# fc2, w1 and w2 of a two-layer image network with seven block products instead of eight (Strassen's method), on one core

## The chip, the cores, the metric

One core of a Trainium2 chip; the program runs on it alone. The metric is the time of one execution on the device, in microseconds (us), of fp32 work throughout. Each run is compared with the kernel before as it ran in the same rounds; from one set of rounds to another that kernel's median lay between 3582.13 and 3584.61 us. The granted clock is the share of full speed that the profile shows for TensorE's clock. A ratio is the mean time of one kernel's fast runs over that of the other's of the same rounds, so it is not quite the ratio of the medians that are quoted.

## What is computed

Eight images of 384 channels and 32x32 pixels pass through two layers: an attention block with a two-matrix MLP, then a ConvNeXt block (7x7 depthwise convolution, layernorm, w1, Gelu, global response normalization GRN, w2). Cut to what matters:

```python
h   = gelu(einsum('bnc,oc->bno', layernorm(x1), w_fc1) + b_fc1)     # 384 -> 1536
x2  = x1 + einsum('bnh,oh->bno', h, w_fc2) + b_fc2                  # fc2: 1536 -> 384
y   = depthwise_7x7(x2);  y = layernorm(y over channels)
y   = gelu(einsum('bhwc,cd->bhwd', y, w1) + b1)                     # w1: 384 -> 1536
gx  = sqrt(sum(y**2 over pixels));  nx = gx / (mean(gx) + eps)
y   = gamma * (y * nx) + beta + y                                   # GRN
out = x2 + einsum('bhwd,dc->bhwc', y, w2) + b2                      # w2: 1536 -> 384
```

## The kernel before

Activations lie with channels on the 128 partitions and 1024 pixels (two halves of 512) along them. A product is one matmul of a 128x128 weight tile with 128x512. Products are written to PSUM tiles of one or two banks; in this program each bank of a tile takes one 128x512 result. fc2, w1 and w2 have 72 such products per image each. A small scheduler (`Flow`) interleaves the instruction streams while the program is written: `flow.pe(us)` tells it how long TensorE will be busy, and side chains (`yield us`) put their next instructions behind so much TensorE work. Every engine then runs its instructions in the order in which they were written; semaphores are set by the framework from what each instruction reads and writes. The stages run in this order for image b: query/key, attention, fc1, fc2 of image b; w1 of image b-1; values of b+1; w2 of b-1. VectorE does the convolution beside all of it.

```python
ps_s = tile_pool("ps_s", bufs=2, PSUM)     # tiles of two banks
ps_o = tile_pool("ps_o", bufs=4, PSUM)     # tiles of one bank
...
def linear(lhsT, rhs, nk, name, done=None):
    ps = ps_s.tile([P, N], F32, tag="s", name=name)          # both halves, two banks
    for k in range(nk):
        for h in range(2):
            nc.tensor.matmul(out=ps[:, half(h)], lhsT=lhsT(k), rhs=rhs(k)[:, half(h)], start=(k == 0), stop=(k == nk - 1))
        flow.pe(2 * U)
    return ps
...
# fc2
for ct in range(CT):
    ps = linear(lambda k: weights.at(wb, k)[:, ct * P : (ct + 1) * P], lambda k: hid[:, k, :], HT, ...)
    nc.vector.scalar_tensor_tensor(xt[:, ct, :], ps, col("bfc2", ct), xt[:, ct, :], ALU.add, ALU.add)
...
# w1
for m in range(HT):
    ps = linear(lambda k: w[:, k, :], lambda k: acc[:, k, :], CT, f"h_{b}_{m}")
    nc.scalar.activation(y[:, m, :], ps, AF.Gelu, bias=b1[:, m : m + 1])
    nc.scalar.activation(ps, y[:, m, :], AF.Square, accum_out=gx[:, m : m + 1])
...
# GRN: the scale goes into w2's rows
nc.scalar.activation(gx, gx, AF.Sqrt)
yield 3.5
nc.tensor.matmul(out=ps[:, :HT], lhsT=ones, rhs=gx, start=True, stop=True)      # gxsum
```

## Time and profile before

| | before |
|---|---|
| median of the runs beside the changed kernel | 3584.61 us (3578.94 to 3587.52, 4 runs) |
| TensorE busy, profiled run | 3498.2 of 3582.0 us, mean granted clock 0.991 |
| one inner image, query/key to query/key | 435.9 us |
| fc2, w1, values, w2 of it | 67.8, 62.7, 16.0, 61.8 us |

The stages are read from the timeline of TensorE: from the first product of one stage to the first of the next. fc2 is longer than w2 because the small column sums of the layernorms stand in it (six or seven of 0.86 us).

### The profile page before, as it was taken

What the parts mean: (1) busy time and instruction counts of PE and PEld (TensorE: products, weight loads), DVE (VectorE), ACT (ScalarE), POOL (GpSimd) and SP (SyncE); (2) the same over time, 40 slices, a digit from 0 to 9 for tenths busy, and PEclk for the clock granted to TensorE, in tenths of its full rate; (3) what the DMA queues carried; (4) which work ended last, traced back from release to release, by engine and by line L of the source; (5) the groups of instructions that cost most, each with busy time, mean ns of one, the idle gap of its engine ahead of it and who ended that gap; (6) DMA issues with size and microseconds to landing.
All of it is one profiled execution on the core that took longest, in us unless ns stands there. A gap on an engine that the chain in (4) does not pass through costs nothing.

```text
span 3582.0 us, 35524 instructions
## 1 busy us (share of the span) xinstructions
PE 3498.2 (98%) x14358; PEld 1475.7 (41%) x14358; DVE 1908.0 (53%) x2151; ACT 1242.5 (35%) x1501; POOL 452.6 (13%) x280
## 2 busy tenths in 40 slices
PE   8999999999999999999999999999999999999978
PEld 3344334443344433444334443444434444344433
DVE  2113795376821768128671376613775247839931
ACT  3541543405424054240542415423153322532130
POOL 1001022100211002200121001120011200224000
PEclk9999999999999999999999999999999999999989
DMA  3012001220012200122002220021201212022110
GB/s 112 13 30 88 17 16 44 84 62 22 16 44 91 61 20 12 50 88 59 19 16 62 72 65 13 24 77 50 65 13 33 89 40 54 16 62 83 53 42 30
DMA packets 93036, 170.56 MB, mean 48 GB/s; under 512 B 29376, under 2 KB 29504, under 8 KB 92736
## 3 DMA queue, kind: packets, MB, share of 16 engines
q1 hardware_dynamic: 92288, 165.73, 16.0%
q8 instruction: 115, 1.88, 0.2%
q10 hardware_dynamic: 576, 2.48, 0.2%
q14 instruction: 57, 0.47, 0.0%
HBM read 133.03 MB, written 25.43 MB: 44 GB/s over the span
## 4 chain that ended last, share of the span: by engine, by line
PE 90%; DVE 7%; POOL 1%; ACT 1%; DMA 0%; issue 0%; SPq 0%; DVEq 0%; POOLq 0%
PE fc L267 13%; PE o L461 12%; PE o L252 12%; PE h L252 12%; PE fc L252 12%; PE s L441 12%; PE qk L252 7%; DVE wqkv L621 5%; PE v L370 4%; PE proj L384 3%; PE ln_var L305 1%; PE ln_sum L290 1%; POOL ln_a L287 1%; DVE acc L621 1%; ACT L274 0%
## 5 line engine op out<-in xcount | busy, mean ns | idle before, releaser
L621 DVE SCALAR_TENSOR_TENSOR acc<-pad,vec,acc 128x1024 f32<-128x1024 f32 x1008 | 1277.1, 1333 | 0.0
L450 ACT ACTIVATE p<-s 128x1024 f32<-128x1024 f32 x512 | 522.6, 1023 | 399.7 <-PE s L441 399.6
L441 PE MATMUL s<-qk 48*64 48x512 f32 x4096 | 537.9, 594 | 12.2 <-ACT p L450 10.7
L461 PE MATMUL o<-p,v 64*64 64x512 f32 x4096 | 533.5, 592 | 0.0
L252 PE MATMUL o<-y,w 128*128 128x512 f32 x1152 | 501.4, 597 | 3.8 <-issue 3.8
L267 PE MATMUL fc<-xn,fc 128*128 128x512 f32 x1152 | 500.6, 593 | 0.0
L252 PE MATMUL fc<-hid,fc 128*128 128x512 f32 x1008 | 441.2, 592 | 0.0
L252 PE MATMUL h<-acc,w 128*128 128x512 f32 x1008 | 437.2, 593 | 0.0
L428 POOL TENSOR_TENSOR attn<-attn,r 128x512 f32<-128x512 f32 x48 | 95.8, 1995 | 1931.5 <-DMA r<-back 1667.2
L252 PEld LDWEIGHTS o<-y,w 128*128 128x128 f32 x1152 | 220.8, 192 | 280.7 <-issue 274.1
L267 PEld LDWEIGHTS fc<-xn,fc 128*128 128x128 f32 x1152 | 218.2, 190 | 278.2 <-issue 273.2
L252 PEld LDWEIGHTS fc<-hid,fc 128*128 128x128 f32 x1008 | 191.5, 190 | 241.1 <-issue 241.1
L252 PEld LDWEIGHTS h<-acc,w 128*128 128x128 f32 x1008 | 190.7, 190 | 235.8 <-issue 235.8
L441 PEld LDWEIGHTS s<-qk 48*64 48x64 f32 x4096 | 153.0, 133 | 308.3 <-issue 273.2
L461 PEld LDWEIGHTS o<-p,v 64*64 64x64 f32 x4096 | 157.1, 133 | 287.8 <-issue 283.5
L546 ACT ACTIVATE hid<-fc,bfc_f 128x512 f32<-128x512 f32 x192 | 131.8, 686 | 372.4 <-PE fc L267 372.3
L354 ACT ACTIVATE qk<-qk,bqk 128x1024 f32<-128x1024 f32 x48 | 53.5, 1114 | 570.9 <-PE qk L252 570.9
L252 PE MATMUL qk<-xn,wqkv 128*128 128x512 f32 x576 | 248.6, 592 | 0.0
L647 ACT ACTIVATE y<-h,b_f 128x1024 f32<-128x1024 f32 x96 | 106.9, 1113 | 290.6 <-PE h L252 257.0
L402 DVE TENSOR_TENSOR attn<-o,attn 128x512 f32<-128x512 f32 x64 | 44.1, 688 | 295.8 <-ACT attn L400 295.8
L621 DVE SCALAR_TENSOR_TENSOR wqkv<-pad,vec,wqkv 128x416 f32<-128x416 f32 (+1 forms) x288 | 191.5, 740 | 0.0
L252 PEld LDWEIGHTS qk<-xn,wqkv 128*128 128x128 f32 x576 | 109.4, 190 | 137.1 <-issue 136.6
(129 smaller groups left out, 1974.9 us busy)
## 6 DMA issues: line engine op xcount, KB each, us to landing
fc<-in_wfc SPq DMA_DIRECT2D x108, 384.0 KB
w<-in_w SPq DMA_DIRECT2D x96, 384.0 KB
xn<-in_x SPq DMA_DIRECT2D x16, 768.0 KB
x<-in_x SPq DMA_DIRECT2D x16, 768.0 KB
kept<-x SPq DMA_DIRECT2D x8, 1536.0 KB
res<-kept SPq DMA_DIRECT2D x48, 256.0 KB
out_y<-res SPq DMA_DIRECT2D x48, 256.0 KB
r<-back SPq DMA_DIRECT2D x96, 96.0 KB
```

Of the source, the lines that this page charges most:

```text
L252: nc.tensor.matmul(out=ps[:, half(h)], lhsT=lhsT(k), rhs=rhs(k)[:, half(h)], start=(k == 0), stop=(k == nk - 1),)
L267: nc.tensor.matmul(out=ps, lhsT=lhsT(k), rhs=rhs(k)[:, half(h)], start=(k == 0), stop=(k == nk - 1))
L354: nc.scalar.activation(parts[:, i, m, :], ps, AF.Identity, bias=bqk[:, at : at + 1], scale=1.0 if i else SCALE)
L370: nc.tensor.matmul(out=ps[:, :C], lhsT=xn[:, k, t * P : (t + 1) * P], rhs=wv_sb[:, k, :], start=(k == 0), stop=(k == CT - 1),)
L384: nc.tensor.matmul(out=ps, lhsT=wproj_sb[:, m, ct * P : (ct + 1) * P], rhs=attn[:, m, :], start=(m == 0), stop=(m == CT - 1),)
L428: nc.gpsimd.tensor_tensor(attn[:, m, :], attn[:, m, :], r, ALU.mult)
L441: nc.tensor.matmul(out=s[64 * i : 64 * i + 64, j, :], lhsT=kT[64 * j : 64 * j + HD, m, k0 : k0 + 64], rhs=qT[64 * j : 64 * j + HD, m, half ...
L450: nc.scalar.activation(p, s, AF.Exp)
L461: nc.tensor.matmul(out=outs[i][64 * j : 64 * j + 64, :], lhsT=v[keys, t, at : at + 64], rhs=p[keys, j, :], start=(t == 0), stop=(t == KT - 1),
L546: nc.scalar.activation(hid[:, m, half(h)], ps, AF.Gelu, bias=bias[:, m : m + 1])
L621: nc.vector.scalar_tensor_tensor(dst, window, tap, dst, ALU.mult, ALU.add)
L647: nc.scalar.activation(y[:, m, :], ps, AF.Gelu, bias=b1[:, m : m + 1])
```

## The change

Two by two blocks are multiplied with seven products in place of eight (Winograd's form): sums of weight blocks S1 to S4 and of activation blocks T1 to T4 are made first, the products are added up after. The third row tile of fc2 and w2 and the third input tile of w1 stay straight. Weight sums of fc2 and w1 are made once in image 0 and kept in DRAM; those of w2 are made for each image, as GRN scales the weights. Done for seven of eight images. T1, T3, T4 are made on GpSimd (for w1 on VectorE), T2 and all sums out of PSUM on VectorE. The core of the diff (exact path, weight order, preparation and pacing cut):

```diff
+    def down(hid, t1, weights, wname, first, add, done, name):          # fc2 and w2
+        def banks(i):
+            ps = ps_s.tile([P, 2, NH], F32, tag="s", name=f"{name}_{i}")
+            return ps[:, 0, :], ps[:, 1, :]
+        straight = banks(0)                                             # A31, A32: 24 products
+        ...
+        making_t3 = flow.spawn(differences(t3, b22, b12), paced=True)   # GpSimd
+        p1, p2 = banks(1)
+        product(p1, "A11", b11)
+        nc.scalar.copy(u2, p1)
+        for k in range(h):
+            nc.vector.tensor_tensor(t2[k], b22[k], t1[k], ALU.subtract)
+        product(p2, "A12", b21)
+        first(0, 0, p2); add(0, 0, u2); done(0, 0)
+        making_t4 = flow.spawn(after(making_t3, differences(t4, b21, t2)), paced=True)
+        p5, p6 = banks(2)
+        product(p5, "S1", t1)
+        first(1, 1, p5); first(0, 1, p5)
+        product(p6, "S2", t2)
+        nc.vector.tensor_tensor(u2, p6, u2, ALU.add)
+        p3, p7 = banks(3)
+        product(p3, "S4", b22)
+        add(0, 1, p3); add(0, 1, u2); done(0, 1)
+        product(p7, "S3", t3)
+        ...
     def grn_up(b, acc, weights, tag, fold):                              # w1, pair (i, j = i + 6)
-            ps = linear(lambda k: w[:, k, :], lambda k: acc[:, k, :], CT, f"h_{b}_{m}")
-            nc.scalar.activation(y[:, m, :], ps, AF.Gelu, bias=b1[:, m : m + 1])
-            nc.scalar.activation(ps, y[:, m, :], AF.Square, accum_out=gx[:, m : m + 1])
+            if fold:
+                fold_b1(i, (a11, a12, a13)); fold_b1(j, (a21, a22, a23))
+            p12 = ps_s.tile([P, 2, NH], F32, tag="s", name=f"h_{b}_{i}")
+            accumulate(p12[:, 0, :], [(a11, b11)])
+            nc.scalar.copy(c21, p12[:, 0, :])
+            accumulate(p12[:, 1, :], [(a13, b31), (a12, b21)])
+            plus(c11, p12[:, 1, :], c21)
+            p5 = product((s1, t1))
+            plus(c21, product((s2, t2)), c21)
+            plus(c12, p5, c21)
+            plus(c12, product((s4, b22), (a13, b32)), c12)
+            finish(i)                                                    # Gelu on ScalarE
+            plus(c21, product((s3, t3)), c21)
+            plus(c22, p5, c21)
+            plus(c21, product((a23, b31), (a22, t4)), c21)
+            plus(c22, product((a23, b32)), c22)
+            finish(j)
+            first_difference(y1, y, i)                                   # T1 of w2, GpSimd
+            for m in (i, j):
+                nc.scalar.activation(squares, y[:, m, :], AF.Square, accum_out=gx[:, m : m + 1])   # squares: p12
-                start_conv(b, 1.55 if b == B - 2 else 1.8)
+                start_conv(b, 1.5 if b == B - 2 else 1.75, 10)
-                    after(state["norm3"], both(xn, xn, eps0, "g1", f"ln1_{b + 1}", True), 0 if b else 6)
+                    after(state["norm3"], both(xn, xn, eps0, "g1", f"ln1_{b + 1}", True, adder=nc.vector), 0 if b else 6)
```

## The prediction

> **What bounds the kernel now.** I read the page first, then the chain of waits, then groups, then the chain in order of time over one inner image. The span and busy lines:
>
> ```profile
> span 3582.0 us, 35524 instructions
> PE 3498.2 (98%) x14358; PEld 1475.7 (41%) x14358; DVE 1908.0 (53%) x2151; ACT 1242.5 (35%) x1501; POOL 452.6 (13%) x280
> PE 90%; DVE 7%; POOL 1%; ACT 1%; DMA 0%; issue 0%; SPq 0%; DVEq 0%; POOLq 0%
> ```
>
> TensorE is busy 98% and holds 90% of the chain that ended last: time is TensorE time. The only long stretch of the chain on VectorE lies near the end (about 3217 to 3441 us, the last image's convolution), which the change leaves as it is. The chain in order of time shows one inner image nearly seamless:
>
> ```profile
> 1107.63 53.22 PE h L252 x124
> 1160.84 3.87 PE v L370 x12
> 1164.71 0.04 issue
> 1164.75 0.39 PE gxsum L662 x2
> 1165.14 11.71 PE v L370 x36
> 1176.86 61.80 PE o L252 x144
> 1238.65 30.91 PE qk L252 x72
> ```
>
> x144 in 61.80 us: one record is 0.429 us, and an fp32 product of 128x128 by 128x512 leaves two records, so it costs **0.858 us**. The image lasts 435.9 us (first query/key product to the next, 802.79 to 1238.65); some 500 such products are 429 us, so only about 7 us are not products. A saved product is worth its whole 0.858 us, as long as nothing new makes TensorE wait; there is hardly any old wait behind which a new one could hide.
>
> [...] The first two lines are VectorE's timeline without and with a GpSimd sum beside it, the third is that sum:
>
> ```profile
> 513.11 2.47 DVE L621 SCALAR_TENSOR_TENSOR acc<-pad,vec,acc 128x1024 f32<-128x1024 f32 x2
> 529.04 3.48 DVE L621 SCALAR_TENSOR_TENSOR acc<-pad,vec,acc 128x1024 f32<-128x1024 f32 x2
> 529.21 2.24 POOL L286 TENSOR_TENSOR ln_a<-x 128x512 f32<-128x512 f32 x1 [4.62 <-DVE x L392]
> ```
>
> Two taps took 2.47 us alone and 3.48 us with it: each GpSimd sum takes 1.0 us from VectorE, and takes itself 2.2 us instead of the 1.3 us of the quiet rows. [...]
>
> ```profile
> L402 DVE TENSOR_TENSOR attn<-o,attn 128x512 f32<-128x512 f32 x64 | 44.1, 688 | 295.8 <-ACT attn L400 295.8
> L286 DVE TENSOR_TENSOR ln_t<-xn 128x512 f32<-128x512 f32 x1 | 0.7, 691 | 12.0 <-DMA xn<-in_x 12.0
> L647 ACT ACTIVATE y<-h,b_f 128x1024 f32<-128x1024 f32 x96 | 106.9, 1113 | 290.6 <-PE h L252 257.0 <-DVE b_f L641 33.5
> L648 ACT ACTIVATE h<-y 128x1024 f32<-128x1024 f32 x96 | 98.6, 1027 | 3.1
> L274 ACT ACT_TABLE_LOAD x47 | 60.3, 1283 | 3.1 <-issue 2.3
> L428 POOL TENSOR_TENSOR attn<-attn,r 128x512 f32<-128x512 f32 x48 | 95.8, 1995 | 1931.5 <-DMA r<-back 1667.2
> L621 DVE SCALAR_TENSOR_TENSOR acc<-pad,vec,acc 128x1024 f32<-128x1024 f32 x1008 | 1277.1, 1333 | 0.0
> ```
>
> In a row I take 0.64 us per sum (three similar ones from L294 stand in 1.87 us). [...] here a load is 1.28 us (L274).
>
> **The change, part by part.**
>
> *Removed.* fc2 goes from 72 products to 66 per image (row tile 2 straight 24, seven block products of 6), w2 likewise, w1 from 72 to 66 (11 instead of 12 for each pair of row tiles, six pairs). Each is done for seven of eight images: fc2 for images 0 to 6, w1 and w2 for 0 to 5 and 7. 3 x 7 x 6 = 126 products x 0.858 = **108 us**, the most there is to win (3.0%).
>
> *w1, VectorE and ScalarE beside it.* A pair now takes 11 x 0.858 = 9.44 us of TensorE. It brings eight VectorE sums out of PSUM (8 x 0.64 = 5.1 us), one ScalarE copy (0.58), two Gelu (1.11 each) and two squares (1.03 + 0.19). By order on each engine they form a loop: copy 0.58, eight sums 5.1, second Gelu 1.11, two squares 2.44, then the next pair's copy: 9.3 us with four handovers of 0.05 us, against 9.44. So TensorE still just leads, with about 0.3 us to spare: of the four banks, the sixth product takes the one that the sum of S2T2 frees about 6.6 us into the pair, and TensorE wants it at 6.87. Four banks are not simply taken in turn (in the attention, two are held while the projection takes three), so p5, held long, need not block. But what norm1 puts into the loop shows: two VectorE sums (1.4 us) and Ln, Exp and two table loads (3.9 us) in the first pair, part of it in idle time. I count 1.5 us for each of six images: **9 us**.
>
> *Wait at the GRN sum.* TensorE issues the gxsum product 3.87 us after w1's last product (lines above). Today ScalarE is just ready: Gelu 1.1, square 1.2, table 1.28, root 0.21 = 3.8. Afterwards: last sum 0.7, Gelu 1.1, two squares 2.4, table 1.28, root 0.21 and handovers = 6.2. New wait 2.4 us x 7 = **17 us**.
>
> *Folding b1, once.* In the first w1 stage each pair now starts with two column sums whose operands VectorE makes (three operations, 1.0 us) after the former pair's last sum: 0.75 + 1.0 + 0.2 + 0.2 + 0.16 + 1.0 + 0.2 = 3.5 us of standing for each of six pairs, 21 us. Folding costs today 9 us (87.6 us from w1's start to w2's in the first image against 78.7 in the next). Net **12 us**. The new preparation of sums in image 0 lies beside an attention with VectorE nearly idle; I allow **3 us**.
>
> *fc2.* GpSimd gets 12 differences (T3, T4), some 1.3 to 2 us each, among norm3's sums; VectorE the six of T2 and 13 sums out of PSUM. The block products wait for nothing: T2 has five microseconds of A12 and five of S1 before it is read, T3 25, T4 30. What can wait is the small layernorm product between them, placed 3 us after its GpSimd sums were issued: the second half's sum of squares falls among T3. I count 2 us for six images: **12 us**.
>
> *w2.* VectorE has per stage of 56.6 us: taps at a pace of 2.28 us (25 x 1.21 = 30 us), seven scalings and sums of 128x768 (0.9 each, 6.3), T2 4.1, thirteen sums 8.7, and 13 us lost to GpSimd: 62 us. It ends some 6 us behind. The banks of S3T3 are what the next stage's first product needs, with 5.1 us between: about 1.2 us x 6 = **7 us**.
>
> *Weights.* 33 loads instead of 24 per image; the page shows DMA engines at 1 to 3 tenths, and w1's tenth chunk is asked for 28 us before its use. Nothing. *Clock:* waits of 1 to 4 us are too short to show here; the granted clock was 0.991.
>
> Sum: 108 - 9 - 17 - 12 - 3 - 12 - 7 = 48 us; 3587 - 48 = **about 3540 us**, 1.3% faster.
>
> **Rivals.** (a) *The loop becomes w1's bound.* If a sum takes its whole 0.69 us and a handover 0.1, the loop is 9.9 us instead of 9.44: another 3 us per stage, and each intrusion counts fully, some 4 us; over seven stages 40 us more. For: the spare time is 0.3 us. Against: neighbours in the trace overlap. It would give 3575 to 3585, no gain. (b) *All is hidden.* The pacing (slow taps at first, norm1's sums moved to VectorE) looks measured; if fc2 and w2 run without a wait and w1 loses only the gxsum wait and the fold, 108 - 29 = 79 us: 3508. For: T2, T3, T4 have slack, and the taps can catch up under the query/key products. Against: two of the terms follow from order alone. (c) [...] With 20 more GpSimd sums under a running convolution, taps end late and norm3 starts late, so fc2 waits: 5 to 10 us an image, 3580 to 3610. Against: 147 taps at a pace of 1.75 us and the slow start make 273 us, and from w1's end to fc2 there are some 293 us of products.
>
> **Range and chances.** The terms I hold firm are 108 saved, 17 and 12 lost. The others (31 us) may vanish or double; (a) adds 40. So 3498 to 3595 for 8 in 10. Below 3515 (2%) needs nearly all of the soft terms to vanish: 0.25. Slower by 2% (3659) would take more than all that is saved plus 72 us: 0.03. Within 2%: 0.72.
>
> **What would show it.** Products on TensorE: 126 fewer, 252 records. w1's stage near 59 to 60 us against 62 (without the layernorm product), its mean idle time released by VectorE; gxsum waits for ScalarE's root by 2.4 us an image; in the first w1 stage, the column sums wait for VectorE, some 20 us in all; w2 57 us with VectorE full and a short wait at the first query/key product. I am wrong if w1 takes over 63 us (rival a), if fc2 waits long for GpSimd or for the end of the convolution (c), or if gxsum and fold waits aren't there.

## The result, and the profile after

The changed kernel takes **3878.89 us** (3875.0 to 3878.92, 4 runs); ratio to the kernel before 1.082, 95% interval 1.0802 to 1.0839. It is 8% slower where I had forecast 1% faster. The page of the changed kernel, busy line and chain by engine:

```profile
span 3877.0 us, 36414 instructions
PE 3534.3 (91%) x14106; PEld 1463.2 (38%) x14106; DVE 2492.5 (64%) x2769; ACT 1262.9 (33%) x1551; POOL 872.5 (23%) x504
PE 75%; DVE 16%; ACT 5%; issue 1%; POOL 1%; DMA 1%; SPq 0%; DVEq 0%; POOLq 0%; ACTq 0%
```

The products are gone as counted: 14358 - 14106 = 252 records. But TensorE is busy for 36 us **longer**, and idle (span less busy) for 343 us instead of 84: 259 + 36 = 295 us. With 108 us of products gone, 36 us longer means that the products that are left take 144 us more than before. VectorE and ScalarE have come onto the chain. What TensorE waited for, longest first in total (the wait, us in total, times, the longest):

```profile
PE h L316 <- ACT y L810: 134.6, 42, 6.1
...
PE o L316 <- DVE res L921: 32.0, 7, 9.9
PE fc L316 <- DVE x L690: 28.9, 7, 4.8
PE b L222 <- DVE w_lnb L218: 24.3, 12, 5.5
PE gxsum L874 <- ACT gx L871: 20.7, 8, 5.7
```

The first line was in no rival of mine. 42 is once for each of the six pairs in each of the seven fast w1 stages. L810 is the copy of the first product. The timeline of all engines around one such wait:

```profile
1175.81 1.02 PE L316 MATMUL h<-acc,w_A 128*128 128x512 f32 x2
...
1181.30 1.03 ACT L828 ACTIVATE h<-y 128x1024 f32<-128x1024 f32 x1
1182.26 0.19 ACT L828 ACTIVATION_READ_ACCUMULATOR h<-y 128x1 f32 x1
1182.35 0.56 ACT L810 COPY y<-h 128x512 f32<-128x512 f32 x1
1182.97 3.78 PE L316 MATMUL h<-acc,w_A 128*128 128x512 f32 x4 [6.14 <-ACT y L810]
```

The first product of the pair (two records) runs at 1175.81. The next two products, which write the *other* bank of the tile p12, start only when ScalarE has copied the first one out, and on ScalarE that copy stands behind the Gelu and both squares of the pair before. And the four records then take 3.78 us where 1.72 would do (4 x 0.43, the kernel before). The granted clock says why; these are stretches of the next pair, with TensorE's busy time first and the clock third from the end:

```profile
1194.40:1198.30 3.90, 0.12 (x1) 0.00 (x0) 0.00 (x0) 3.81 (x6) 0.00 (x0) 0.83 0.39 101
1198.30:1202.00 3.70, 3.69 (x5) 1.62 (x6) 0.00 (x0) 0.00 (x0) 0.00 (x0) 0.50 0.00 0
1202.00:1206.00 4.00, 4.00 (x9) 1.77 (x8) 1.91 (x3) 0.00 (x0) 0.00 (x0) 0.78 0.00 0
1206.00:1210.00 4.00, 4.00 (x10) 1.74 (x10) 3.03 (x6) 1.15 (x1) 1.27 (x1) 1.00 0.36 96
```

A wait of 3.8 us, then the clock at half for the products after it. Of the 30 waits for the copy of 3.8 us and more, 28 are followed by the half clock (0.50 to 0.57 over the next 3.4 us) and two (ending at 1229.45 and 2181.78) are not (1.00). The mean granted clock fell from 0.991 to 0.954. As time: (1 - 0.991) x 3582 = 32 us lost before, (1 - 0.954) x 3877 = 178 us after; the difference, 146 us, fits the 144 us by which the products got longer. So the wait is paid twice, as idle time and as slow products; that is how TensorE can be busy longer with 108 us less work. Shorter waits come up under e6 to e8.

The same pattern is in fc2 and w2: `fc L316 <- DVE x L690` and `o L316 <- DVE res L921`, seven times each, are the sixth product waiting for the readers of the fifth, its neighbour in one tile. In fc2 these readers stand on VectorE behind the six differences of T2, which run while GpSimd makes differences of T3 (VectorE's timeline of the changed kernel):

```profile
1117.69 9.09 DVE L654 TENSOR_TENSOR hid<-hid,fc_t 128x512 f32<-128x512 f32 x6
```

9.09 us for six, against 3.69 us for six in a w2 stage of the same run (from 1297.73, where GpSimd stood still for the first 2 us). In the kernel before, two taps took 2.47 us alone and 3.48 us with a GpSimd sum beside them (the prediction shows both), which goes the same way; that GpSimd is the cause of the 9.09 us is my estimate, as no run here separates it. In the stages of one inner image:

| us | fc2 | w1 | values | w2 | whole image |
|---|---|---|---|---|---|
| before | 67.8 | 62.7 | 16.0 | 61.8 | 435.9 |
| after | 73.0 | 90.5 | 17.8 | 64.6 | 475.2 |

28 of the 39 us are in w1.

### The profile page after: what moved, and what is told of

It reads as the page before. It is cut to its first block, busy times and chain, and to the rows that moved or that the text cites. A ratio compares the mean times of both kernels' runs of the same rounds, so it can differ in the third digit from the quotient of the medians.

```text
span 3877.0 us, 36414 instructions
## 1 busy us (share of the span) xinstructions
PE 3534.3 (91%) x14106; PEld 1463.2 (38%) x14106; DVE 2492.5 (64%) x2769; ACT 1262.9 (33%) x1551; POOL 872.5 (23%) x504
## 4 chain that ended last, share of the span: by engine, by line
PE 75%; DVE 16%; ACT 5%; issue 1%; POOL 1%; DMA 1%; SPq 0%; DVEq 0%; POOLq 0%; ACTq 0%
PE fc L309 12%; PE h L316 11%; PE o L507 10%; PE s L487 10%; PE qk L296 6%; PE o L316 5%; DVE wqkv L770 5%; PE fc L316 4%; PE o L627 4%; PE fc L627 4%; PE proj L430 3%; PE v L416 3%; DVE acc L770 3%; ACT h L828 2%; DVE hid L654 1%
## 5 line engine op out<-in xcount | busy, mean ns | idle before, releaser
L770 DVE SCALAR_TENSOR_TENSOR acc<-pad,vec,acc 128x1024 f32<-128x1024 f32 x1008 | 1338.0, 1386 | 0.0
L804 DVE TENSOR_TENSOR y<-h,y 128x512 f32<-128x512 f32 x336 | 231.7, 691 | 360.8 <-PE h L316 357.4
L474 POOL TENSOR_TENSOR attn<-attn,r 128x512 f32<-128x512 f32 x48 | 107.2, 2233 | 1256.6 <-DMA r<-back 1029.2
L316 PE MATMUL h<-acc,w_A 128*128 128x512 f32 x432 | 270.6, 740 | 114.4 <-ACT y L810 114.4
L807 ACT ACTIVATE y<-y,b_f 128x1024 f32<-128x1024 f32 x84 | 96.4, 1148 | 406.4 <-DVE y L804 406.3
L645 POOL TENSOR_TENSOR y<-y 128x512 f32<-128x512 f32 x84 | 174.5, 2110 | 75.4 <-PE o L316 64.4
L600 POOL TENSOR_TENSOR w_t<-y 128x512 f32<-128x512 f32 x42 | 55.8, 1330 | 596.6 <-ACT y L807 596.6
L316 PEld LDWEIGHTS h<-acc,w_A 128*128 128x128 f32 x432 | 94.4, 230 | 248.0 <-ACT y L810 148.7
L316 PE MATMUL o<-y,w_S 128*128 128x512 f32 x252 | 121.9, 642 | 38.1 <-DVE res L921 32.0
```

Source lines behind the costliest of these rows:

```text
L316: nc.tensor.matmul(out=bank, lhsT=lhsT, rhs=rhs, start=k == 0, stop=k == len(pairs) - 1)
L645: nc.gpsimd.tensor_tensor(dst[k], one_[k], other[k], ALU.subtract)
L770: nc.vector.scalar_tensor_tensor(dst, window, tap, dst, ALU.mult, ALU.add)
L804: nc.vector.tensor_tensor(dst, bank, part, ALU.add)
```

## The experiments

Theory A: the framework's dependence is by tile. A product that writes one bank of a two-bank tile waits for a reader of the other bank that stands before it in the program. Rival B: the loop of sums, Gelu and squares on VectorE and ScalarE is simply longer than a pair's products (my rival a). A third question is how much the clock adds.

### e1: the copy later (w1)

```diff
             accumulate(p12[:, 0, :], [(a11, b11)])
-            nc.scalar.copy(c21, p12[:, 0, :])
             accumulate(p12[:, 1, :], [(a13, b31), (a12, b21)])
+            nc.scalar.copy(c21, p12[:, 0, :])
```

> Edit: in the w1 stage the ScalarE copy of the first product (bank 0 of the two-bank PSUM tile) is issued after the two products for bank 1, not before them. Data and arithmetic stay. Theory A (a product that writes one bank of a two-bank tile is made to wait for the reader of the other bank, so the copy, which stands behind the former pair's squares on ScalarE, closes a loop through TensorE): the wait of h products for the copy (42 times, 134.6 us on TensorE's own queue, and slow clock after it) goes; a w1 stage falls from some 90 us to 60 to 64, the whole from 3879 to about 3690 (3660 to 3720). Rival B (the loop of VectorE sums, Gelu and squares is simply longer than a pair's products, wherever the copy stands): w1 stays above 80 us, the whole above 3820.

Measured: 3682.76 us, ratio to before 1.0278 (1.0261 to 1.0295). w1's stage is 62.0 us instead of 90.5; the wait for L810 is gone from the list; the mean clock is 0.978. One line moved, with no arithmetic changed, gives back 196 of 294 us. Rival B would have left it above 3820; it falls as the main cause.

### e2: readers of the first product after the second (fc2, w2)

```diff
         product(p1, "A11", b11)
-        nc.scalar.copy(u2, p1)
         ...                                    # T2
         product(p2, "A12", b21)
+        nc.scalar.copy(u2, p1)
 ...
         product(p5, "S1", t1)
-        first(1, 1, p5); first(0, 1, p5)
         product(p6, "S2", t2)
+        first(1, 1, p5); first(0, 1, p5)
 ...                                            # and the sums of p3 after product(p7)
```

> Edit: in fc2 and w2 alone, for each of the three tiles that hold two block products, the readers of the first product are issued after the second product (copy of P1 after P2, first sums of P5 after P6, sums of P3 after P7). Theory A: the waits of the second product for VectorE and ScalarE go (in the trace 39 us for fc2's L316 products, 43 us for w2's, and slow clock after them); fc2 falls from 79 us to about 70, w2 from 65 to about 60: whole 3790 to 3830. Rival ([...]): fc2 and w2 change by less than 2 us each, the whole stays above 3850.

Measured: 3790.42 us, ratio 1.0580 (1.0562 to 1.0598). fc2 is 66.7 us instead of 73.0, w2 56.7 instead of 64.6. Within what theory A expected; the rival falls: T2's data did not hold the sixth product. Own tiles (as in e12 below) were not tried in fc2 and w2, so that it is the tile there too is taken over from w1.

### e3: both orders

> Both edits. Theory A: the gains add, about 190 + 70: 3580 to 3640. If all that my prediction missed was this one wait, it comes near the predicted 3540 (below 3570). Rival B: above 3800.

Measured: 3593.48 us, ratio 1.0031 (1.0015 to 1.0048). The gains add: 196 + 88 = 284 of the 294 us, 285 measured. With the waits by tile gone, the change costs and gains nothing on balance, and 53 us are missing to my 3540. TensorE's busy time is 3422.8 us for the same 14106 records, 112 us less than in the changed kernel. TensorE's list of waits in e3, without its two largest lines of old waits:

```profile
PE gxsum L874 <- ACT gx L871: 24.7, 8, 6.3
PE b L222 <- DVE w_lnb L218: 24.2, 12, 5.4
PE ln_sum L336 <- DVE ln_a L333: 16.8, 7, 2.5
PE ln_var L351 <- POOL ln_sq L348: 11.8, 8, 3.1
...
PE h L316 <- DVE y L804: 8.5, 6, 1.7
PE ln_var L351 <- DVE ln_sq L348: 7.6, 6, 1.5
```

Most are terms that the prediction had: the GRN sum, the fold, the sums of squares in fc2, and w1's loop. The column sum of norm1 that waits for VectorE (`ln_sum <- DVE ln_a`) it had not. So the wait by tile was not all that the prediction missed: by e3's own expectation that would have been below 3570.

### e4: w1 straight, fc2 and w2 in the mended order

```diff
-        # seven products per block, as above
+        for m, tiles in ((i, (0, 1, 2)), (i + HT // 2, (5, 3, 4))):
+            ps = linear(lambda k: raw[:, tiles[k], :], lambda k: acc[:, k, :], CT, f"h_{b}_{m}")
+            nc.scalar.activation(y[:, m, :], ps, AF.Gelu, bias=b1[:, m : m + 1])
+            nc.scalar.activation(ps, y[:, m, :], AF.Square, accum_out=gx[:, m : m + 1])
```

> fc2 and w2 with seven products, readers of the first product issued after the second as in e2; w1 undone: straight with eight (twelve per pair of row tiles) in all images, Gelu and squares from PSUM as in the kernel before. By my prediction's terms 84 products are saved, 72 us, less 12 (fc2), 7 (w2), 3 (preparation): about 3535 (3510 to 3570). If the fast w1 is worth nothing even in the good order, e4 is not slower than e3; if it is worth its 36 us, e4 is slower than e3 by 10 to 36.

Measured: 3548.17 us, ratio 0.9896 (0.9879 to 0.9913): 1% faster than before, and 45 us faster than e3. The part with the most new waits is better undone, at this point.

### e12: own tiles, old order

The decisive test between "the place of the copy" and "the shared tile": the changed kernel as it is, but the second and third product get a bank of their own.

```diff
             accumulate(p12[:, 0, :], [(a11, b11)])
             nc.scalar.copy(c21, p12[:, 0, :])
-            accumulate(p12[:, 1, :], [(a13, b31), (a12, b21)])
-            plus(c11, p12[:, 1, :], c21)
+            plus(c11, product((a13, b31), (a12, b21)), c21)
```

> The changed kernel with its order (copy of the first product before the second bank's products), but the second and third product go into a one-bank tile of their own instead of the second bank of the tile that the copy reads. Theory A (sharing a tile makes the wait, not the place of the copy): the wait goes as in e1, 3670 to 3710. Rival (it was the order: ScalarE must have done the copy for some other reason before TensorE can go on): 3840 to 3880.

Measured: 3686.01 us, ratio 1.0285 (1.0267 to 1.0304), w1's stage 62.0 us: the same as e1 with the copy at its old place. It is the shared tile that makes the wait. Two different banks alone don't ask for it: in e12 TensorE's timeline shows no wait from 1166.39 to 1206.64, so each copy of that time (0.56 us in the changed kernel's trace) ran beside its products, and the result is correct.

### e5: products more, to fill the wait

```diff
             nc.scalar.copy(c21, p12[:, 0, :])
+            idle = o_tile(f"idle_{b}_{i}")
+            for _ in range(4):
+                nc.tensor.matmul(out=idle, lhsT=a11, rhs=b11, start=True, stop=True)
```

> The changed kernel as it is, and in each of the 42 pairs of w1 four products more (3.4 us each pair at full clock, result unused) between the first product and the ones that wait for the copy. In the trace of the changed kernel that wait is 3.8 to 6.1 us and the granted clock after it is 0.50 for some 3.5 us. Clock theory: TensorE is no longer idle in the wait, keeps its clock, and 168 products more make the kernel faster, by 42 x about 1.7 = 40 to 75 us: 3800 to 3840, mean clock from 0.954 to 0.97 or more. Rival (the wait is all, the low clock hardly matters): no gain, 3879 or up to 40 us more.

Measured: 3836.48 us, ratio 1.0708 (1.0691 to 1.0726): **42 us faster with 168 products more**, mean clock 0.976 instead of 0.954. What is left of the wait for the copy, in TensorE's list:

```profile
PE h L316 <- ACT y L810: 22.6, 30, 2.7
```

At full clock the 168 products are 144 us of work (0.858 us each), and the wait shrank by 112 us (134.6 to 22.6). By that alone the kernel would be 32 us slower: 12 of the 42 waits were short, and four products did not fit into them. That it is 42 us faster is the clock, which therefore gave some 74 us (an estimate: 42 + 32). It agrees roughly with the lost clock time, 178 us before and (1 - 0.976) x 3832 = 92 us now. The gain was at the lower end of what the clock theory expected.

### e6, e7, e8: the GRN sum later, the fold earlier, both (on e3)

The fold: the layernorm's shift times w1 is added to b1 once, by column sums on TensorE that stand in the first w1 stage.

```diff
         nc.scalar.activation(gx, gx, AF.Sqrt)      # e6
-        yield 3.5
+        yield 7.0
-                y, y1, gx = grn_up(b - 1, acc, weights, b - 1, b == 1)      # e7: b1 is folded in prepare()
+                y, y1, gx = grn_up(b - 1, acc, weights, b - 1, False)
```

> Both orders mended (as e3) and the small gxsum product issued some 7.7 us after w1's last product instead of 3.9, behind two more value products. In e3 TensorE waited 24.7 us for it (8 times) against 7.8 in the kernel before, and the trace shows the clock at half for 3.4 us behind six of these waits. Theory: 17 us of wait and up to 10 us of slow clock go: 3593 to 3565 to 3577. Rival (the wait moves to w2's start, because the scales come later): no change.

> Both orders mended (as e3) and the folding of b1 moved from the first w1 stage to the preparation in image 0 (weights loaded once more there, six loads). In e3 the column sums waited 24.2 us for VectorE in that stage and the clock lost some 17 us there. Theory: 35 to 42 us gained, less some in image 0: 3593 to 3550 to 3565. Rival (image 0 can't take it; its attention waits for VectorE or the load queue instead): 3580 or more.

> e6 and e7 together, on both orders. If the terms are independent they add: 3593 - 22 - 38 = about 3533 (3520 to 3545), faster than the kernel before by some 1.4%, and faster than e4, which has w1 straight (3548): then the fast w1 does pay once the three waits that it brought are gone.

Measured: e6 3578.81 us (ratio 0.9986, 0.9969 to 1.0003), e7 3562.17 us (0.9942, 0.9926 to 0.9959), e8 3548.49 us (0.9905, 0.9889 to 0.9922). So mending the GRN sum gained 15 us, the fold 31, and they add. (In e6's trace the value stages of the six inner images are some 24 us shorter in all than in e3's; fc2's stages took back 1.5 to 1.7 us in three of these images. Why stays open.) e8 missed its 3533: against e3 it won 45 us, not 60, and is level with e4, not better. In e3 each inner wait for the GRN sum but the first is 2.45 to 2.81 us, and the clock falls after it, in five of five (TensorE's timeline, then a stretch after it):

```profile
1196.16 0.39 PE L874 MATMUL gxsum<-gx,ones 128*128 128x12 f32 x2 [2.45 <-ACT gx L871]
```

```profile
1196.00:1200.00 4.00, 3.83 (x8) 2.21 (x9) 3.16 (x8) 0.86 (x3) 0.00 (x0) 0.58 0.00 0
```

The length of a wait does not settle it, though. The six waits of 2.46 us in e3's fc2 stages (`ln_sum <- DVE ln_a`) are as long; the clock fell after one of them and stayed at 1.00 after the other five. The 4 us after that one, and after the next image's:

```profile
1104.45:1108.45 4.00, 4.00 (x6) 1.76 (x7) 1.89 (x3) 1.11 (x2) 3.52 (x3) 0.57 0.00 0
1539.21:1543.21 4.00, 4.00 (x10) 1.85 (x11) 1.89 (x3) 2.05 (x4) 3.53 (x3) 1.00 0.00 0
```

In the kernel before, three of the eight waits of 1.25 us at the start of the attention were followed by a lower clock (0.53 to 0.62 over the next 3.6 us, e.g. 0.57 from 1273.09 to 1276.50), and five by 1.00. What decides was not tested.

### e9, e10: longer pauses in the layernorm chains (on e8 and e4)

```diff
         adder.tensor_tensor(a, a, src[:, 2, cols], ALU.add)
-        yield 3.2
+        yield 3.2 if name[:3] != "ln1" else 6.0
 ...
-        yield 3.0
+        yield 3.0 if name[:3] != "ln3" else 4.5
```

> e8 with two pauses in the layernorm chains longer (norm1's column sum is issued 6.0 us after its VectorE sums instead of 3.2, norm3's sum of squares 4.5 us after its GpSimd sums instead of 3.0). In e8 TensorE waited 16.8 us for norm1's VectorE sums, 11.8 us for GpSimd and 10.8 us for VectorE at the sums of squares. Theory (these are the waits that took back fc2's gain: its stage took 68 us, as before the change, instead of 62.6): 3548 to 3520 to 3535. Rival (the layernorm ends later and the w1 stage or the value products wait instead): no gain.

> e4 (w1 straight, orders mended) with the same two longer pauses. Theory: as in e9, 15 to 25 us gained: 3548 to 3523 to 3533. Against e9 it shows what the fast w1 is worth when all its waits known so far are mended: by the stages of e8 (62.3 us against 62.7 before) nothing, within 10 us.

Measured: e9 **3521.20 us**, ratio 0.9826 (0.9809 to 0.9844); e10 **3521.58 us**, ratio 0.9823 (0.9806 to 0.9841). Both are 1.7 to 1.8% faster than the kernel before, and level with each other. fc2's stage fell from 68.4 us (e8, where it is 66.7 or 68.4 by image) to 61.8: the waits of the layernorm products had eaten the whole gain there. Of this 0.86 us is no gain: with the longer pauses one small layernorm product stands in w1's stage instead of fc2's, which is why w1 is longer in the last two rows of the table below. The profiled execution of e9 was the fastest of its four (3513.03 us, the others 3520 to 3524), that of e10 the slowest (3525.42), so their stages must not be set against each other to a microsecond.

### e11: w2 alone

fc2 and w1 straight, norm1's sums on GpSimd again, preparation cut to w2's part.

> Only w2 with seven products (order mended); fc2 and w1 straight, norm1's sums on GpSimd as in the kernel before, no preparation but w2's. w2's stage took 57 us in e8 against 61.8 before, fc2's as long as before. Theory: 7 x 4.5 = 31 us less than before, and image 0 loses little: 3550 to 3560, as good as e4, because fc2 fast gave nothing there. Rival (fc2 fast pays in e4): slower than e4 by 10 us or more.

Measured: 3552.83 us, ratio 0.9914 (0.9896 to 0.9932). w2 alone gives as much as e4, so in e4 the fast fc2 paid next to nothing, as its stage said (66.7 us against 67.8, less what image 0 pays for the preparation). With e10's pauses it does pay: e10 is 31 us faster than e11. The pauses could not have gained this with fc2 straight, as e11's fc2 stage has no wait (67.8 us is 72 products and seven small ones).

| inner image, us | fc2 | w1 | values | w2 | whole |
|---|---|---|---|---|---|
| before | 67.8 | 62.7 | 16.0 | 61.8 | 435.9 |
| after | 73.0 | 90.5 | 17.8 | 64.6 | 475.2 |
| e1 | 73.0 | 62.0 | 18.4 | 64.8 | 447.5 |
| e3 | 68.4 | 62.0 | 20.1 | 56.7 | 434.7 |
| e8 | 68.4 | 62.3 | 15.7 | 56.7 | 430.7 |
| e9 | 61.8 | 63.0 | 15.7 | 56.7 | 426.5 |
| e10 (w1 straight) | 61.8 | 63.5 | 16.0 | 56.6 | 427.9 |

## Why the prediction was wrong

**The first step that failed** stands in the part on w1 and the one on fc2. "TensorE still just leads" took the copy to be off TensorE's path: I let TensorE be held only by free banks and operands. "The block products wait for nothing" said the same of fc2. In the program that was built, the second product of a shared tile waits for the copy of the first, so a loop that I had drawn through VectorE and ScalarE alone closed through TensorE: products, sums, Gelu, two squares, copy, next products, one after the other. e1 and e12 show it from two sides: 196 and 193 us. The same in fc2 and w2 is 88 us (e2). What warned me was in reach: both products are halves of one `tile([P, 2, NH])` in the diff, and the kernel before never reads one half while it still writes the other, so its trace could not show what happens then.

**The second step that failed** was one sentence: "waits of 1 to 4 us are too short to show here". Of the 30 long waits for the copy (3.8 us and more) 28 were followed by the half clock, and so were the five inner waits of 2.45 to 2.81 us for the GRN sum in e3. By the stretches shown above, the clock was at half for some 3.4 us after a wait of 2.45 us (e3; an estimate: 0.42 x 4.00 us over 0.50) and for some 6.8 us in all around one of 3.8 us (an estimate in the same way, from the three stretches from 1194.40 to 1206.00). It made the difference of 146 us in lost clock time; e5 shows it by itself. The trace of the kernel before had it already: after a wait of 2.74 us in the first w1 stage it shows

```profile
721.40:724.80 3.40, 3.40 (x10) 2.49 (x11) 1.93 (x4) 1.30 (x2) 0.00 (x0) 0.50 0.36 139
```

**The other steps, by their size.** The 126 products are gone (252 records). The wait at the GRN sum was right in mechanism and size: 24.7 us in e3 against 7.8 before is 17, as predicted; mending it gave 15, clock included. The fold was right in mechanism (24.2 us of waits, 21 predicted) but mis-sized: taking it out gained 31 us in e7, what image 0 pays for it included, where 21 were expected (12 net of the 9 that folding cost before). The clock is at half after most of its waits (0.50 after 661.54 and 682.04 in e3, for instance). fc2's layernorm waits: the mechanism was right, the term was 2 us an image, measured 4.1 to 5.8 (66.7 to 68.4 us in e3, less 62.6 for 66 products and seven small ones); I had only the GpSimd half, and norm1's VectorE sums (16.8 us in e3) were the larger one. w1's stage: 1.5 us an image expected for what norm1 puts into it, measured 62.0 - 57.5 = 4.5 in e3 (57.5 is 66 products and one small one). About 3.1 of it are two waits in the first two pairs (1.48 us for norm1's squares, 1.66 us for a bank), some 1 us is the loop itself. For the loop, the prediction's sum was wrong as it stands: its terms, 0.58 + 5.1 + 1.11 + 2.44 and four times 0.05, make 9.43 us, not 9.3, so there never was anything to spare against 9.44. Eight sums in a row took 5.73 us, 0.72 each, not the 0.64 that I took (VectorE's timeline of e3, two pairs):

```profile
1146.92 5.73 DVE L804 TENSOR_TENSOR y<-h,y 128x512 f32<-128x512 f32 x8 [3.91 <-ACT y L811]
1156.56 5.72 DVE L804 TENSOR_TENSOR y<-h,y 128x512 f32<-128x512 f32 x8 [3.91 <-ACT y L811]
```

The loop as measured is 1156.56 - 1146.92 = 9.64 us a pair, against 9.44 of products; rival (a) was right that the loop bounds w1, but by 0.2 us a pair, which is not the result. The preparation: attention and what lies in it took 140 us in image 0 instead of 131, 8 us where I allowed 3 (changed kernel); the chain that ended last passes there through the load queue: the stores of the sums, then the attention's own small transfer (`sums<-attn`, 4.59 us at 130.31). w2's term was 1.2 us an image; in e3 its stage is 56.7 us, which is 66 products. In e3's list no wait of an inner image names the convolution or a load, so rival (c) fell.

**Where the gain went, then.** 108 us of products; in e9 63 us of it remain. Of the fast w1 nothing remains: e9, which has it, and e10, which has it not, are level. In e9's profiled run its stage is 61.9 to 63.0 us where 66 products and two small ones are 58.3. About 2 us of this are one wait for a bank behind norm1's work on VectorE (2.06 us, once an image); after three of the six such waits the clock fell too (0.60 from 1106.74 to 1110.74), and where it did not, the pairs that follow take the loop's 9.63 us (686.62 to 696.26 and on to 705.89). The mean granted clock is lower in all of e9's runs (0.984 to 0.987) than in e10's (0.988 and 0.989). What the preparation takes, and how the last 45 us split, I did not measure.

## What to carry to other kernels

When two accumulations share one tile of two banks, issue both before any reader of the first, or give each its own tile: otherwise a reader on a busy engine holds TensorE back (here 42 waits of up to 6.1 us between two different banks of one tile; own tiles made the kernel 193 us faster, e12). On a kernel that lives from a TensorE without gaps, count each new wait as idle time and allow for slow products after it (here after 28 of 30 waits of 3.8 us and more, after one of six of 2.46 us, after three of eight of 1.25 us), and look for the loop through all engines, not for the sum on each. Saved products are worth their time only after the small products between them, which wait for other engines, have been moved back too (here ratio 1.0031 in e3, 0.9826 in e9).
